# Mamba layer of a four-layer hybrid: in 4 of 16 channel pairs the scan's inputs go through ScalarE and GpSimd, and its decays stay in PSUM

## The chip, the cores and the metric

The kernel runs on one core of a Trainium2 chip. A core has a tensor engine (PE, which does matmuls into PSUM), a vector engine (DVE), a scalar engine (ACT, ScalarE), GpSimd (POOL) and a sync engine (SP) that issues the DMAs here. Each works through its own list of instructions in order, and they wait for one another through semaphores. The metric is the device time of one execution, in microseconds (us).

## The reference, cut to what matters

A tensor x of 4 images, 56 x 56 positions, 128 channels passes four layers: neighbourhood attention, Mamba, additive attention with experts, and dense attention with experts. The change lies in the second, the Mamba layer. It treats every image row as a sequence of 56 steps and runs two blocks one after the other:

```python
u = silu(conv4(h @ in_w[:, :256]));  res = h @ in_w[:, 256:]     # 256 channels
dt, Bm, Cm = split(u @ xw, [8, 24])                              # 8, 16, 16
delta = softplus(dt @ dtw + dtb);  A = -exp(A_log)               # A: 256 x 16 states
dA  = exp(delta[t, d] * A[d, n])                                 # the decays
dBu = delta[t, d] * u[t, d] * Bm[t, n]                           # the inputs
h_t = dA * h_{t-1} + dBu;  y[t, d] = sum_n h_t[d, n] * Cm[t, n] + D * u
out = (y * silu(res)) @ ow
```

So for each of 256 channels and 16 states there is a scan over time, with decays dA and inputs dBu.

## The kernel before, in words

`layer1` cuts an image into 7 chunks of 448 positions (8 rows of 56). A block is one chunk in one of the two Mamba blocks (l = 0 or 1): 4 images x 7 chunks x 2 = 56 blocks, in `order`: four chunks with l = 0, the same four with l = 1, then the other three likewise.

In a block, 256 channels x 16 states are 4096 scans, 128 at a time on the partitions (8 channels x 16 states), with two such groups side by side in one tile of 128 x 896. That is a *pair*; a block has 16 (`PAIRS`), and there are 896 in all. The work of a pair p:

- `decays` (L723): two matmuls with the matrix `A_pick` spread delta of 8 channels over 128 partitions and multiply by A, into the PSUM tile `a` (one buffer).
- ScalarE takes the Exp of `a` into the SBUF tile `E` (L748, three buffers).
- `spread_inputs` (L732): two matmuls with `pick` spread delta * u likewise into the PSUM tile `u` (two buffers).
- `inputs` (L753): DVE multiplies `u` in place, in PSUM, by B (`bc[:, 0]`).
- `scan` (L760): DVE scans over time with E (SBUF) and u (PSUM) into the SBUF tile `hs` (seven buffers). The decay at a row's first position is 0, because delta there was set very large (L939), so that rows don't mix.
- POOL multiplies `hs` in place by C (L765).
- `sums` (L771): PE adds up the 16 states into the PSUM tile `y`, for two pairs at once, in odd steps, up to five steps later.

The order on PE, ScalarE, DVE and POOL is that of the program text: `manual_schedule` leaves it as written. The main loop goes over p; what one pass issues is this:

```python
for step in first.get(p, []): step()
if p >= -2: select(p + 1)            # decays of p+2, inputs of p+1, Exp of p+2
if 0 <= p < n_pairs: scan(p)
if p % 2 and 0 <= p - 5 < n_pairs: sums(p - 5)
for step in last.get(p, []): step()
inputs(p + 1)
```

`first` and `last` hold the rest of the work, placed at fixed passes of the 16 of a block. The preparation of the next block (`mamba_pre`) is spread over the present one: convolution matmuls (L889) in passes 14, 15, 0 and 1, their copies out of PSUM (L897) first in passes 0 and 2; both Silu (L901) last in pass 2, which needs another activation table and so costs a table load before and one after; the projection to dt, B, C (L907) in pass 3; its copy (L913) and four spreading matmuls (L918) in passes 4 to 7 with their copies (L924, L929); the Softplus (L932), again between two table loads, last in pass 6; delta * u on POOL (L936) in pass 8; the residual branch (L943, L951) in passes 9 to 11. The end of a block lies in the next: the gate (L786 on ScalarE, L787 on POOL) in pass 11 and in pass 3 of the next block, the output projection (L796 for l = 0, L804 for l = 1) last in pass 8, and its copy to h (L814) or addition to X (L820, DVE) in pass 9. At three of the four images' ends, group-norm work for the next image is put in as well (L184, L194 to L229, L247).

What the change touches is `select`, `inputs` and the loop.

Of the kernel before, what the change touches and what calls it, by code (L numbers as in the profile page):

```python
# [11 lines left out]
AF = mybir.ActivationFunctionType  # L12
# [8 lines left out]
P = 128  # L21
# [3 lines left out]
CH = TC * TP  # L25
# [11 lines left out]
DBL = DR + 2 * DS  # L37
QG = 4
PAIRS = DI // 16
LONG = 1.0e30  # L40

AH = 16
# [63 lines left out]
class Hybrid:  # L106
# [570 lines left out]
    def layer1(self):  # L677
# [3 lines left out]
        nc, a, tc = self.nc, self.a, self.tc  # L681
        ET = mybir.EngineType
        with ExitStack() as ctx:
            w = self.w1
            big = ctx.enter_context(tc.tile_pool(name="l1_big", bufs=1))
            sm = ctx.enter_context(tc.tile_pool(name="l1_sm", bufs=2))
            ps_m = ctx.enter_context(tc.tile_pool(name="l1_m", bufs=1, space=PSUM))
            ps_a = ctx.enter_context(tc.tile_pool(name="l1_a", bufs=1, space=PSUM))
            ps_u = ctx.enter_context(tc.tile_pool(name="l1_u", bufs=2, space=PSUM))
# [11 lines left out]
            ]  # L701
            n_pairs = PAIRS * len(order)
            h = {}
            pre, yg, E, V, HS, py = {}, {}, {}, {}, {}, {}
# [5 lines left out]
            def place(p):  # L710

                j, i = divmod(p, PAIRS)
                return j, i // 8, i // 2 % 4, i % 2 * 2


            two_banks = lambda pool, tag: self.t(pool, [P, 1024], tag)[:, 512 - CH : 512 + CH]
            halves = lambda t: t.rearrange("p (k q) -> p k q", k=2)

            def decays(p, to):
                j, f, q, r0 = place(p)  # L720
                for k in range(2):
                    own = slice((r0 + k) * HD, (r0 + k + 1) * HD)
                    nc.tensor.matmul(  # L723
                        halves(to)[:, k], w["A"][own, order[j][2], f, q, :], pre[j]["delta"][own, f],
                        start=True, stop=True,
                    )

            def spread_inputs(p, to):
                j, f, q, r0 = place(p)
                for k in range(2):  # L730
                    own = slice((r0 + k) * HD, (r0 + k + 1) * HD)
                    nc.tensor.matmul(  # L732
                        halves(to)[:, k], w["pick"][own, q, :], pre[j]["du"][own, f],
                        start=True, stop=True,
                    )

            def select(p):
                if 0 <= p + 1 < n_pairs:  # L740
                    t = two_banks(ps_a, "a")
                    decays(p + 1, t)
                if 0 <= p < n_pairs:
                    V[p] = two_banks(ps_u, "u")
                    spread_inputs(p, V[p])
                if 0 <= p + 1 < n_pairs:
                    E[p + 1] = self.t(sm, [P, 2 * CH], "E", bufs=3)
                    nc.scalar.activation(E[p + 1], t, AF.Exp)  # L748

            def inputs(p):  # L750
                if 0 <= p < n_pairs:
                    v = halves(V[p])
                    nc.vector.tensor_mul(  # L753
                        v, v, pre[p // PAIRS]["bc"][:, 0:1].to_broadcast([P, 2, CH])
                    )


            def scan(p):
                flat = self.t(sm, [P, 2 * CH], "hs", bufs=7)
                nc.vector.tensor_tensor_scan(  # L760
                    flat, E.pop(p), V.pop(p), 0.0, op0=ALU.mult, op1=ALU.add
                )
                HS[p] = halves(flat)
                bc = pre[p // PAIRS]["bc"]
                nc.gpsimd.tensor_mul(HS[p], HS[p], bc[:, 1:2].to_broadcast([P, 2, CH]))  # L765

            def sums(p):

                j, f, q, _ = place(p)
                for r in range(4):  # L770
                    nc.tensor.matmul(  # L771
                        py[j, f][r * HD : (r + 1) * HD, :], w["sum"][:, q, :], HS[p + r // 2][:, r % 2],
                        start=False, stop=(q == QG - 1),
                    )
# [51 lines left out]
            for j, block in enumerate(order):  # L826
                at = PAIRS * j
                if j and block[1:] == (0, 0):

                    g = self.group_norm(block[0], big, w["group"])  # L830
                    for c in range(NCH):
                        to = at - (5 - c // 3) * PAIRS + 11 + c % 3
                        add(last, to, g.turn, c, m)
# [30 lines left out]
            for p in range(-PAIRS - 2, n_pairs + PAIRS):  # L864
                for step in first.get(p, []):
                    step()
                if p >= -2:
                    select(p + 1)
                if 0 <= p < n_pairs:
                    scan(p)  # L870
                if p % 2 and 0 <= p - 5 < n_pairs:
                    sums(p - 5)
                for step in last.get(p, []):
                    step()
                inputs(p + 1)

    def mamba_pre(self, pre, j, block, h, w, sm, m):

# [55 lines left out]
        def du():  # L934
# [3 lines left out]
            for f in range(NHALF):  # L938
                nc.gpsimd.memset(seqs(r["delta"][:, f])[:, :, 0:1], LONG)  # L939

# [996 lines left out]
```

## Time and profile before

| | |
|---|---|
| time, median of 3 runs | 7885.04 us (7883.99 to 7885.86) |
| span of the profiled execution, first to last instruction | 7883.1 us |
| what the median has beyond that span | 1.9 us |
| Mamba stage, first to last scan | 650.8 to 3531.3 us |
| DVE scans L760 | 896, mean 2020 ns |
| DVE products L753 | 896, mean 1076 ns |
| ScalarE Exp L748 | 896, mean 917 ns |
| POOL products L765 | 896, mean 2084 ns |
| mean granted TensorE clock, whole span | 0.949 of full speed |

The profile shows one execution. An engine's busy time is the sum of its instructions' durations; a group's line gives busy time and mean duration, then the idle time of the engine just before those instructions and what ended most of it. A timeline line is start, duration, engine, line, operation, output <- inputs, shapes, count, and in brackets the idle time before it and its releaser. A windows line is a stretch, its length, the busy time (and instructions) of PE, PE's weight loads, DVE, ACT and POOL, the granted TensorE clock, and the share and rate of the DMA.

### The profile page before, as it was taken

The numbers are of one execution on the slowest core, as the hardware profiler recorded it, in microseconds if no ns is written. First come the engines' busy times: TensorE is split into PE (matmuls) and PEld (weight loads), VectorE is DVE, ScalarE is ACT, GpSimd is POOL, SyncE is SP. The second block draws the span as 40 slices with busy tenths as digits, with TensorE's granted clock in tenths as the row PEclk, the third lists the DMA queues.
The fourth block names the chain that finished last, engine by engine and source line by source line (L and its number), as shares of the span: only waits on it lengthen the run. The fifth ranks groups of instructions, "written<-read, shape, count | busy, mean of one in ns | idle before, by whom it ended". The sixth has DMA issues, their size and how long they took to land.

```text
span 7883.1 us, 105890 instructions
## 1 busy us (share of the span) xinstructions
PE 6718.3 (85%) x41081; PEld 2672.6 (34%) x41081; DVE 6070.7 (77%) x10241; ACT 4990.0 (63%) x4903; POOL 2552.6 (32%) x1911
## 2 busy tenths in 40 slices
PE   7888989998999899987777777777777889999999
PEld 3452333333333333322222222222222344444544
DVE  5787999999999999997877887877787755344434
ACT  4455555555555655548998899899889953333332
POOL 4455777777777777760000000000001000000000
PEclk8998999999999999999999999899999989999999
DMA  3000000000000000000000000000003101210000
GB/s 63 6 2 1 1 1 1 1 1 1 1 1 1 1 1 1 1 3 2 1 1 1 5 1 1 1 5 1 1 32 114 47 6 47 91 57 5 5 5 6
DMA packets 86479, 102.35 MB, mean 13 GB/s; under 512 B 21368, under 2 KB 51414, under 8 KB 85463
## 3 DMA queue, kind: packets, MB, share of 16 engines
q1 hardware_dynamic: 85975, 95.58, 4.2%
q8 instruction: 322, 5.28, 0.3%
q14 instruction: 182, 1.49, 0.1%
HBM read 85.28 MB, written 10.29 MB: 12 GB/s over the span
## 4 chain that ended last, share of the span: by engine, by line
PE 35%; DVE 33%; ACT 20%; issue 7%; POOL 1%; DVEq 0%; DMA 0%; ACTq 0%; SPq 0%; POOLq 0%
DVE hs L760 17%; ACT th L1149 13%; PE q L1707 7%; PE o L1718 7%; DVE u L753 6%; PE s L1160 6%; DVE th L1140 4%; PE o L1187 2%; PE pe L1872 2%; ACT E L748 2%; PE a L723 2%; PE m L889 2%; DVE e L488 1%; ACT L748 1%; PE y L771 1%
## 5 line engine op out<-in xcount | busy, mean ns | idle before, releaser
L1149 ACT ACTIVATE th<-th 128x3136 f32<-128x3136 f32 (+12 forms) x1120 | 2293.6, 2093 | 194.6 <-DVE th L1140 138.4
L1140 DVE TENSOR_SCALAR th<-fT,g 128x784 f32<-128x784 f32 (+6 forms) x3920 | 1918.4, 556 | 482.2 <-PE s L1160 449.9
L765 POOL TENSOR_TENSOR hs<-hs,bc 128x896 f32<-128x896 f32 x896 | 1867.3, 2084 | 793.5 <-DVE hs L760 761.3
L1160 PE MATMUL s<-th,place 128*32 128x392 f32 (+7 forms) x14336 | 1489.2, 492 | 667.8 <-ACT th L1149 664.8
L760 DVE TENSOR_TENSOR_SCAN hs<-E,u 128x896 f32<-128x896 f32 x896 | 1810.1, 2020 | 117.9 <-ACT E L748 1.9
L748 ACT ACTIVATE E<-a 128x896 f32<-128x896 f32 x896 | 821.5, 917 | 806.3 <-PE u L732 333.7
L723 PE MATMUL a<-delta,A_pick 32*128 32x448 f32 x3584 | 983.2, 601 | 148.0 <-ACT E L748 140.4
L753 DVE TENSOR_TENSOR u<-u,bc 128x896 f32<-128x896 f32 x896 | 964.2, 1076 | 63.9 <-PE u L732 63.5
L732 PE MATMUL u<-du,pick 32*128 32x448 f32 x3584 | 975.2, 601 | 35.8 <-DVE hs L760 35.7
L1160 PEld LDWEIGHTS s<-th,place 128*32 128x32 f32 (+1 forms) x14336 | 425.7, 111 | 1612.1 <-ACT th L1149 1082.4
L1712 ACT ACTIVATE e<-q,shift 128x448 f32<-128x448 f32 (+1 forms) x700 | 441.4, 633 | 748.6 <-PE q L1707 748.2
L1178 POOL TENSOR_TENSOR e<-e,later 112x112 f32<-112x112 f32 x112 | 80.2, 716 | 2311.9 <-ACT e L1171 1670.1
L1718 PE MATMUL o<-e,xk 128*128 128x448 f32 (+1 forms) x1400 | 653.1, 548 | 25.7 <-ACT oT L1693 25.7
L1877 DVE SCALAR_TENSOR_TENSOR X<-pe,r_gate,X 112x128 f32<-112x128 f32 x896 | 314.0, 351 | 455.3 <-PE pe L1872 419.7
L1707 PE MATMUL q<-xT 128*128 128x448 f32 (+1 forms) x1400 | 654.7, 550 | 2.3 <-ACT e L1712 2.2
L723 PEld LDWEIGHTS a<-delta,A_pick 32*128 32x128 f32 x3584 | 295.7, 188 | 697.4 <-ACT E L748 466.5
L771 PE MATMUL y<-hs,sum 128*32 128x448 f32 x3584 | 443.9, 566 | 4.4 <-POOL hs L765 4.4
L1187 PE MATMUL o<-e,xa 112*128 112x392 f32 (+5 forms) x1024 | 424.3, 537 | 1.1 <-POOL e L1178 1.1
L1718 PEld LDWEIGHTS o<-e,xk 128*128 128x128 f32 (+1 forms) x1400 | 262.2, 191 | 310.5 <-issue 275.5
L732 PEld LDWEIGHTS u<-du,pick 32*128 32x128 f32 x3584 | 295.5, 188 | 200.0 <-DVE hs L760 183.9
L1707 PEld LDWEIGHTS q<-xT 128*128 128x128 f32 (+1 forms) x1400 | 249.0, 189 | 238.1 <-issue 213.0
L1806 POOL MEMSET lc_xa<- 112x4 f32 x28 | 3.1, 110 | 889.5 <-DVE lc_xa L1800 519.5
(254 smaller groups left out, 7186.2 us busy)
## 6 DMA issues: line engine op xcount, KB each, us to landing
wide<-in_L_ffn_weight SPq DMA_DIRECT2D x64, 1024.0 KB
X<-in_x SPq DMA_DIRECT2D x8, 784.0 KB
out<-X SPq DMA_DIRECT2D x28, 224.0 KB
M<-wide SPq DMA_DIRECT2D x4, 784.0 KB
wide<-M SPq DMA_DIRECT2D x4, 784.0 KB
e_edge<-dtab SPq DMA_DIRECT2D x42, 49.0 KB
cw<-in_L_conv_conv_w SPq DMA_DIRECT2D x4, 256.0 KB
c_h<-in_L_ffn_weight SPq DMA_DIRECT2D x16, 64.0 KB
```

Of the source, the lines that this page charges most:

```text
L723: nc.tensor.matmul(halves(to)[:, k], w["A"][own, order[j][2], f, q, :], pre[j]["delta"][own, f], start=True, stop=True,)
L732: nc.tensor.matmul(halves(to)[:, k], w["pick"][own, q, :], pre[j]["du"][own, f], start=True, stop=True,)
L748: nc.scalar.activation(E[p + 1], t, AF.Exp)
L753: nc.vector.tensor_mul(v, v, pre[p // PAIRS]["bc"][:, 0:1].to_broadcast([P, 2, CH]))
L760: nc.vector.tensor_tensor_scan(flat, E.pop(p), V.pop(p), 0.0, op0=ALU.mult, op1=ALU.add)
L765: nc.gpsimd.tensor_mul(HS[p], HS[p], bc[:, 1:2].to_broadcast([P, 2, CH]))
L1140: nc.vector.tensor_scalar(th[i][:, blk, lo:hi], fT[j][:, lo:hi], im[order[j][0]]["g"][:, at : at + 1], None, op0=ALU.add,)
L1149: nc.scalar.activation(own, own, AF.Tanh)
L1160: nc.tensor.matmul(ps[j, J][QW * blk : QW * blk + rows, h, lo:hi], place[:, off : off + rows], z[:, blk, h * HALF + lo : h * HALF + hi], s ...
L1187: nc.tensor.matmul(po[j][:, h, lo:hi], im[b]["xa"][:, J, :], e[:, h * HALF + lo : h * HALF + hi], start=(J == 0), stop=(J == t + ((h + 1) ...
L1707: nc.tensor.matmul(ps[:n, :CH], xT[b][:, k : k + n], xT[b][:, c * CH : (c + 1) * CH], start=True, stop=True,)
L1718: nc.tensor.matmul(po[b, c], xk[b][:n, t, :], es.pop((b, c, t))[:n], start=(t == 0), stop=(t == N - 1))
```

## The change

For the pairs 0, 3, 7 and 12 of every block (`POOL_PAIRS`) the two PSUM tiles change their contents. The pair's inputs go, one pass earlier than before, into `a`; ScalarE copies them to a new SBUF tile `V` (two buffers), and POOL multiplies V by B. Its decays go, one pass later than before, into `u`; ScalarE takes their Exp in place, in PSUM, and the scan reads them there, with V as its inputs. In ScalarE's order that Exp stands before the copy or Exp of the following pair; in POOL's order the product stands before the C product of the pair scanned in that pass. The other 12 pairs are as before.

```diff
+POOL_PAIRS = (0, 3, 7, 12)
...
+            on_pool = lambda p: p % PAIRS in POOL_PAIRS
+
             def select(p):
-                if 0 <= p + 1 < n_pairs:
+                far, near = p + 1, p
+                if 0 <= far < n_pairs:
                     t = two_banks(ps_a, "a")
-                    decays(p + 1, t)
-                if 0 <= p < n_pairs:
-                    V[p] = two_banks(ps_u, "u")
-                    spread_inputs(p, V[p])
-                if 0 <= p + 1 < n_pairs:
-                    E[p + 1] = self.t(sm, [P, 2 * CH], "E", bufs=3)
-                    nc.scalar.activation(E[p + 1], t, AF.Exp)
-
-            def inputs(p):
-                if 0 <= p < n_pairs:
+                    (spread_inputs if on_pool(far) else decays)(far, t)
+                if 0 <= near < n_pairs:
+                    u = two_banks(ps_u, "u")
+                    (decays if on_pool(near) else spread_inputs)(near, u)
+                    if on_pool(near):
+                        E[near] = u
+                        nc.scalar.activation(u, u, AF.Exp)
+                    else:
+                        V[near] = u
+                if 0 <= far < n_pairs:
+                    if on_pool(far):
+                        V[far] = self.t(sm, [P, 2 * CH], "V")
+                        nc.scalar.copy(V[far], t)
+                    else:
+                        E[far] = self.t(sm, [P, 2 * CH], "E", bufs=3)
+                        nc.scalar.activation(E[far], t, AF.Exp)
+
+            def inputs(p, eng):
+                if 0 <= p < n_pairs and on_pool(p) == (eng is nc.gpsimd):
                     v = halves(V[p])
-                    nc.vector.tensor_mul(
+                    eng.tensor_mul(
                         v, v, pre[p // PAIRS]["bc"][:, 0:1].to_broadcast([P, 2, CH])
                     )
...
                     select(p + 1)
+                    inputs(p + 2, nc.gpsimd)
...
-                inputs(p + 1)
+                inputs(p + 1, nc.vector)
```

## The prediction

> **What bounds the kernel now.** I read the engine totals first, then the groups of instructions, then the scan stage alone, then its timeline block by block. The page (its last column is idle time and who ended it):
>
> ```profile
> span 7883.1 us, 105890 instructions
> ...
> L765 POOL TENSOR_TENSOR hs<-hs,bc 128x896 f32<-128x896 f32 x896 | 1867.3, 2084 | 793.5 <-DVE hs L760 761.3
> ...
> L760 DVE TENSOR_TENSOR_SCAN hs<-E,u 128x896 f32<-128x896 f32 x896 | 1810.1, 2020 | 117.9 <-ACT E L748 1.9
> L748 ACT ACTIVATE E<-a 128x896 f32<-128x896 f32 x896 | 821.5, 917 | 806.3 <-PE u L732 333.7
> ...
> L753 DVE TENSOR_TENSOR u<-u,bc 128x896 f32<-128x896 f32 x896 | 964.2, 1076 | 63.9 <-PE u L732 63.5
> ```
>
> The Mamba stage is the 896 pairs (56 blocks of 16), from 650 to 3531 us. Its windows row (busy time of each engine, then the granted TensorE clock):
>
> ```profile
> 650.00:3531.00 2881.00, 2621.89 (x13355) 906.74 (x13354) 2742.93 (x1876) 1616.29 (x1968) 2103.30 (x1202) 0.96 0.00 1
> ```
>
> DVE is busy 95%, so it looks like the bound; but PE is busy 91%. The reader should distrust both shares and look for the loop that closes from one block to the next. I call "step p" the loop pass that selects pair p+1 and scans pair p, counted 0 to 15 in a block. The timeline of one block, PE first; the bracket is idle time before:
>
> ```profile
> 1537.70 1.02 PE L723 MATMUL a<-delta,A_pick 32*128 32x448 f32 x4 [1.00 <-ACT E L748]
> ...
> 1540.81 1.77 PE L907 MATMUL m<-us,xw 128*128 128x448 f32 x4 [0.49 <-ACT us L901]
> 1543.04 0.64 PE L723 MATMUL a<-delta,A_pick 32*128 32x448 f32 x2 [0.46 <-ACT E L748]
> ...
> 1555.22 0.65 PE L723 MATMUL a<-delta,A_pick 32*128 32x448 f32 x2 [1.22 <-ACT E L748]
> ...
> 1556.18 1.77 PE L796 MATMUL m<-yg,ow 128*128 128x448 f32 x4
> ```
>
> From step 2 to step 8 PE waits for ScalarE, whose order there is: E, table load, two silu, table load, E (steps 2 and 3); E, table load, softplus, table load, E (steps 6 to 8):
>
> ```profile
> 1536.73 0.92 ACT L748 ACTIVATE E<-a 128x896 f32<-128x896 f32 x1 [0.33 <-PE u L732]
> 1537.67 1.28 ACT L901 ACT_TABLE_LOAD   x1
> ...
> 1549.34 0.92 ACT L748 ACTIVATE E<-a 128x896 f32<-128x896 f32 x1
> 1550.27 1.28 ACT L932 ACT_TABLE_LOAD   x1
> ```
>
> And another block, where the same projection ran at half the granted clock (3.16 us, not 1.77) and DVE then waited for pair 10:
>
> ```profile
> 778.82:782.23 3.41, 3.41 (x8) 1.28 (x11) 3.28 (x3) 0.80 (x1) 2.46 (x2) 0.50 0.00 0
> ```
> ```profile
> 778.59 3.16 PE L796 MATMUL m<-yg,ow 128*128 128x448 f32 x4
> ```
> ```profile
> 783.07 1.10 DVE L753 TENSOR_TENSOR u<-u,bc 128x896 f32<-128x896 f32 x1 [0.30 <-PE u L732]
> ```
>
> Taking start times in the timeline for every block, the loop from the step-2 matmuls of one block (1535.67 above) to those of the next is a sum of five parts:
> - step 2 to step 8 on PE and ScalarE: 19.55 us in 52 of 55 blocks, 20.20 in three;
> - step 8 to pair 10's u in PSUM (the projection lies here): 3.70 to 3.93 us at full clock, on average 5.60 where the clock was 0.5;
> - slack until DVE starts pair 10's product: 0.1 or 1.0 to 2.1;
> - DVE from there to the end of scan 14: 15.80 (five pairs at 3.14);
> - scan 14's end to the next step 2: 0.05, then 9.83 of PE (L732, L771, L889 back to back).
>
> With slack 1.36: 19.55 + 3.70 + 1.36 + 15.80 + 0.05 + 9.83 = 50.29, the measured period, which is 16 x 3.14: DVE is the bound. Of the 43 blocks without group-norm work, 25 (all with a slow projection) have slack 0.1 and last 51.09; 18 have 1.49 and last 50.65; mean 50.91. So two bounds are about equally tight: DVE, and a loop PE - ScalarE - PE - DVE - PE.
>
> **The change, part by part**, for the pairs 0, 3, 7, 12 of each block.
>
> *DVE product removed, 4 a block.* Scan to scan is now 3.14 us; without the product a scan can follow at 1.94 (start to start, the distance at which a product follows a scan in the rows) plus 0.03: 1.17 saved each, 224 x 1.17 = 262 us if DVE alone mattered. Which of these count? Only pair 12 lies in the DVE part of the loop (pairs 10 to 14): -1.17. Pair 0 comes after scan 14, where PE needs 9.83 us while DVE's three pairs took 9.42 already: nothing. Pairs 3 and 7 lie between steps 2 and 8, where PE and ScalarE set the pace; DVE arrives earlier at pair 10 and waits there. That is the slack, 1.49 us in the 18 blocks, nothing in the 25.
>
> *Exp of the near pair added on ScalarE, 4 a block.* PSUM to PSUM has no row here; I bound it by 0.83 (start to start of back-to-back rows of that width) and 0.95 (L901, SBUF to SBUF); a gain is excluded, since it is one more instruction on an engine that works in order. I take 0.92, the E row, nearest in function and shape: the next one starts 0.83 later. The changed program's order on ScalarE puts it ahead of E and of the table load in step 2 (pair 3) and step 6 (pair 7). In step 2, E moves by 0.83, and with it the table load, silu, L907, everything to step 8. In step 6 ScalarE has 0.19 us idle to give: +0.64. Together +1.47 on the 19.55. In step 11 (pair 12) it moves a(14) by 0.8, but u(13) is ready 0.7 before DVE wants it; in step 15 (pair 0) E(17) ends 0.7 before PE wants its bank. Both free; without that cover they cost up to 0.8 more a block.
>
> *Copy of the far pair's inputs in place of an Exp.* L951 copies half the width in 0.53, so between 0.53 and 1.06; I take 0.90 like E: nothing changes, no table load is added (Copy runs between E rows already).
>
> *Product on POOL added.* 2.08 by L765. POOL per block: 16 x 2.084 + 2.09 + 2 x 1.13 + 0.3 = 38.0, new 46.3 of about 51. Each V product stands in POOL's queue before the preceding C product, so behind it wait those products and, four steps later, PE's sums. Pair 12's: the copy ends 3.8 to 4.4 after pair 10's u is ready (where E of pair 12 ends now, in the two kinds of block), the product at 5.9 to 6.5, scan 11 at 6.5 to 6.7: in time by 0.2 to 0.6. Pairs 0, 3, 7 by 0.5 or more. I take 0; if POOL ran 0.1 us longer per product the lag of six would cost up to 0.6.
>
> *Matmuls* are exchanged, not added, on the same row groups as now; no DMA is touched. *Scan* with its decays in PSUM and inputs in SBUF: no row; the rows reach 1.959 to 2.023, I take 2.02, +-0.06. DVE and POOL each read one SBUF tensor as before; L765 is 2071 to 2111 ns over all 896 beside a DVE 95% busy. [...]
>
> *Sum per block.* Unhindered: 50.65 - 1.49 + 1.47 - 1.17 = 49.46, plus 0.3 in the half of the blocks with L796 (pair 11 then waits for h: 16.10 in the rows, not 15.80), mean 49.6. With the slow projection: 51.09 + 1.47 - 1.17 = 51.39. The share of slow projections decides. Slow stretches follow stretches in which PE idled (above, 0.50 right after the 1.2 us wait), and the change adds 0.83 and 0.64 us of such idling, so I expect more than 25 of 43; I take 85%: 51.12, +0.21 x 43 = +9. [...]
> Slow steps 3 and 4, not seen now, would cost 0 to 0.8 a block (L907 1.77 longer, less the 0.49 and 0.46 that PE waits around it); nearest to none today, so 0.1 taken: +5. The 12 group-norm blocks: in nine PE is 0.4 to 2.1 late behind scan 14, so pair 12's gain is partly lost: +0.8 x 12 = +10. The last block has no successor and is DVE's: -4. Total +20: 7883.1 + 20 = 7903 for the span, and with the 1.9 us by which the median exceeds the span, **7905**.
>
> **Rivals.**
> 1. *DVE bound throughout*: -262 us, 7623. For it: 95% busy. Against: the slack list; DVE already stops at pair 10 in 25 of 43 blocks.
> 2. *Faster (other side)*: the new rhythm leaves the half-clock stretches away from the projection. At none: 43 x (49.6 - 50.91) = -56, +10, -4: 7835; it decides from a share under about 45%. For it: runs of blocks without one (1316 to 1513). Against: more PE idling.
> 3. *Nothing measurable*: the share stays 25 of 43: 50.65, -11, +10, -4: 7880.
> 4. *Much slower*: POOL's lag reaches the scans or steps 3 and 4 run at half clock: +0.6 to 0.8 a block, 7930 to 7955.
>
> **How the numbers follow.** Forecast (share 70 to 100%) 0.42, rival 1 0.02, rival 2 0.20, rival 3 0.22, rival 4 0.14. 0.2% is 16 us, about what a measurement can tell here. The forecast's own range, 7890 to 7925, crosses that line (7901): a sixth of its chance, 0.07, counts as same. Of rival 3, 0.20 is same and 0.02 faster. Faster 0.02 + 0.20 + 0.02 = 0.24, same 0.27, slower 0.35 + 0.14 = 0.49. The range: 7850 (rival 2 nearly whole) to 7950 (rival 4).
>
> **What would show it.** Right: DVE's idle time before L760 and L753 rises together from 182 to about 440 us, at pairs 4, 5 and 10; DVE about 2500 us busy in the stage, POOL 2570; step 2 to step 8 near 21.0; PE idle before L723 for ScalarE up by about 80 us. Wrong: a step 2 to step 8 still at 19.6, or a period near 46 us. The prediction falls if the near Exp finds idle time I missed, or if the clock's half-speed stretches change their number.

## The result, and the profile after

The changed kernel takes 7937.02 us (median; 7936.14 to 7937.26), the kernel before 7885.45 us (7883.99 to 7893.94) in the same comparison: a ratio of 1.0064, with a 95% interval of 1.0049 to 1.0078. It is slower by 51.6 us where the prediction said 20. That is inside the predicted range, but above the forecast's own 7890 to 7925, among the times that rival 4 had (7930 to 7955).

The page of the changed kernel: the span, then the groups that answer to those shown of before (mean ns of one instruction, then the engine's idle time just before, and who ended it).

```profile
span 7935.0 us, 106227 instructions
...
L778 POOL TENSOR_TENSOR hs<-hs,bc 128x896 f32<-128x896 f32 x896 | 1847.7, 2084 | 80.9 <-DVE hs L773 76.9
L773 DVE TENSOR_TENSOR_SCAN hs<-E,u 128x896 f32<-128x896 f32 x672 | 1357.7, 2020 | 68.8 <-DVE u L766 1.4
L724 PE MATMUL a<-delta,A_pick 32*128 32x448 f32 x2688 | 765.5, 614 | 290.9 <-ACT E L761 278.8
...
L766 DVE TENSOR_TENSOR u<-u,bc 128x896 f32<-128x896 f32 x672 | 727.4, 1082 | 278.2 <-PE u L733 276.8
...
L766 POOL TENSOR_TENSOR V<-V,bc 128x896 f32<-128x896 f32 x224 | 466.8, 2084 | 246.7 <-ACT V L758 246.2
L773 DVE TENSOR_TENSOR_SCAN hs<-u,V 128x896 f32<-128x896 f32 x224 | 449.9, 2008 | 88.2 <-ACT u L752 88.0
...
L752 ACT ACTIVATE u<-u 128x896 f32<-128x896 f32 x224 | 202.0, 902 | 219.1 <-PE u L724 209.5
```

Its windows row for the Mamba stage (length, busy time of PE, weight loads, DVE, ACT and POOL, then the granted TensorE clock):

```profile
644.60:3573.00 2928.40, 2505.17 (x13354) 857.68 (x13352) 2532.69 (x1653) 1787.31 (x2191) 2538.36 (x1425) 0.94 0.00 1
```

DVE has 210 us less work in the stage than before, and the stage is 48 us longer (2928.4 against 2880.6 us). DVE's idle time before its products and scans went from 182 to 435 us (68.8 + 278.2 + 88.2), and most of it ends with PE's `u`. (Some 45 us on either side is a single wait, before the stage's first pair.) No DVE wait of weight names POOL. PE's wait for `E` doubled, 140 to 279 us.

The loop of five parts, mean of the 43 plain blocks, from start times in the timelines:

| | step 2 to 8 | 8 to u(10) | slack | product 10 to end of scan 14 | to next step 2 | period |
|---|---|---|---|---|---|---|
| before | 19.55 | 4.86 | 0.69 | 15.92 | 9.88 | 50.91 |
| after | 21.40 | 5.41 | 0.14 | 14.65 | 9.77 | 51.37 |

The 12 group-norm blocks went from 53.48 to 55.94. So 43 x 0.46 = 20 and 12 x 2.46 = 30 us came in the blocks; with the edges of the stage (the last block is 2 us shorter) that is its 48 us, and all else in the program adds 4. That 4 is not explained: the part behind the stage, the same code in all of them, lasts 4350 to 4372 us in the profiles of the fourteen kernels here.

Step 2 to step 8 takes 21.29 us in the 40 blocks with a slow projection, 1.74 more than before; in the other three steps 3 and 4 ran at half clock (there L921 took 3.35 or 3.36 us instead of 1.77), and they raise the mean to 21.40. Where the 1.74 us came from, in one block's timeline (start, duration, engine, line; in brackets idle time before and its releaser). PE first, from step 3 to the projection:

```profile
1545.63 0.65 PE L724 MATMUL a<-delta,A_pick 32*128 32x448 f32 x2 [1.87 <-ACT E L761]
...
1548.73 1.77 PE L921 MATMUL m<-us,xw 128*128 128x448 f32 x4 [1.18 <-ACT us L915]
...
1559.10 0.64 PE L724 MATMUL a<-delta,A_pick 32*128 32x448 f32 x2 [0.89 <-ACT E L761]
...
1565.23 3.17 PE L809 MATMUL m<-yg,ow 128*128 128x448 f32 x4
```

ScalarE in the same block, steps 2 and 6:

```profile
1543.85 0.90 ACT L752 ACTIVATE u<-u 128x896 f32<-128x896 f32 x1 [0.39 <-PE u L724]
1544.67 0.91 ACT L761 ACTIVATE E<-a 128x896 f32<-128x896 f32 x1
1545.60 1.28 ACT L915 ACT_TABLE_LOAD   x1
...
1557.32 0.90 ACT L752 ACTIVATE u<-u 128x896 f32<-128x896 f32 x1 [0.18 <-PE a L724]
1558.13 0.91 ACT L761 ACTIVATE E<-a 128x896 f32<-128x896 f32 x1
1559.07 1.28 ACT L946 ACT_TABLE_LOAD   x1
```

The near Exp (L752) stands ahead of E and of the table load both times. PE's wait for E in step 2 is 1.87 where before had 1.00. In step 6 the near Exp itself waits, by the profile, for matmuls into the other tile, `a` (0.18 us, in 55 of the 56 blocks): the matmuls of the two tiles are interleaved and the last of `a` are late (they alternate with L932), so ScalarE's idle time, which I had counted as cover, isn't there.

And DVE, which waits at pairs 3, 5, 9 and 10:

```profile
1544.86 2.02 DVE L773 TENSOR_TENSOR_SCAN hs<-u,V 128x896 f32<-128x896 f32 x1 [0.66 <-ACT u L752]
...
1552.09 1.10 DVE L766 TENSOR_TENSOR u<-u,bc 128x896 f32<-128x896 f32 x1 [2.09 <-PE u L733]
...
1565.37 1.10 DVE L766 TENSOR_TENSOR u<-u,bc 128x896 f32<-128x896 f32 x1 [1.92 <-PE u L733]
...
1569.45 1.10 DVE L766 TENSOR_TENSOR u<-u,bc 128x896 f32<-128x896 f32 x1 [0.86 <-PE u L733]
```

The projection L809 took 3.17 us, not 1.77. Windows rows of that stretch: PE was busy 1.67 of 3.42 us, and the next stretch, with the projection, was granted 0.50.

```profile
1561.25:1564.67 3.42, 1.67 (x10) 0.60 (x10) 2.11 (x2) 3.10 (x5) 3.42 (x3) 1.00 0.01 2
1564.67:1568.08 3.41, 3.41 (x8) 1.17 (x4) 2.60 (x2) 0.92 (x1) 3.23 (x4) 0.50 0.00 0
```

This holds in 40 of the 43 plain blocks, against 25 before.

### The profile page after: what moved, and what is told of

The parts are those of the page before. It is cut to its first block, busy times and chain, and to the rows that moved or that the text cites. A ratio compares the mean times of both kernels' runs of the same rounds, so it can differ in the third digit from the quotient of the medians.

```text
span 7935.0 us, 106227 instructions
## 1 busy us (share of the span) xinstructions
PE 6600.8 (83%) x41081; PEld 2622.1 (33%) x41081; DVE 5859.5 (74%) x10017; ACT 5163.7 (65%) x5127; POOL 2989.2 (38%) x2135
## 4 chain that ended last, share of the span: by engine, by line
PE 52%; ACT 27%; DVE 13%; issue 7%; DMA 0%; POOL 0%; ACTq 0%; DVEq 0%; SPq 0%; POOLq 0%
ACT th L1163 13%; PE q L1721 7%; PE o L1732 7%; PE a L724 6%; PE s L1174 6%; DVE th L1154 5%; PE m L903 5%; ACT E L761 4%; PE o L1201 3%; PE pe L1886 2%; PE y L784 2%; DVE e L489 2%; PE a L733 2%; ACT u L752 2%; ACT L761 2%
## 5 line engine op out<-in xcount | busy, mean ns | idle before, releaser
L1174 PE MATMUL s<-th,place 128*32 128x392 f32 (+8 forms) x14336 | 1494.1, 494 | 672.0 <-ACT th L1163 668.8
L778 POOL TENSOR_TENSOR hs<-hs,bc 128x896 f32<-128x896 f32 x896 | 1847.7, 2084 | 80.9 <-DVE hs L773 76.9
L773 DVE TENSOR_TENSOR_SCAN hs<-E,u 128x896 f32<-128x896 f32 x672 | 1357.7, 2020 | 68.8 <-DVE u L766 1.4
L724 PE MATMUL a<-delta,A_pick 32*128 32x448 f32 x2688 | 765.5, 614 | 290.9 <-ACT E L761 278.8
L766 DVE TENSOR_TENSOR u<-u,bc 128x896 f32<-128x896 f32 x672 | 727.4, 1082 | 278.2 <-PE u L733 276.8
L761 ACT ACTIVATE E<-a 128x896 f32<-128x896 f32 x672 | 615.4, 916 | 375.5 <-PE u L733 363.7
L733 PE MATMUL u<-du,pick 32*128 32x448 f32 x2688 | 758.0, 615 | 5.4 <-DVE hs L773 5.3
L766 POOL TENSOR_TENSOR V<-V,bc 128x896 f32<-128x896 f32 x224 | 466.8, 2084 | 246.7 <-ACT V L758 246.2
L773 DVE TENSOR_TENSOR_SCAN hs<-u,V 128x896 f32<-128x896 f32 x224 | 449.9, 2008 | 88.2 <-ACT u L752 88.0
L724 PEld LDWEIGHTS a<-delta,A_pick 32*128 32x128 f32 x2688 | 228.2, 189 | 750.1 <-ACT E L761 534.8
L752 ACT ACTIVATE u<-u 128x896 f32<-128x896 f32 x224 | 202.0, 902 | 219.1 <-PE u L724 209.5
```

The costliest lines, as they stand in the source:

```text
L724: nc.tensor.matmul(halves(to)[:, k], w["A"][own, order[j][2], f, q, :], pre[j]["delta"][own, f], start=True, stop=True,)
L733: nc.tensor.matmul(halves(to)[:, k], w["pick"][own, q, :], pre[j]["du"][own, f], start=True, stop=True,)
L761: nc.scalar.activation(E[far], t, AF.Exp)
L766: eng.tensor_mul(v, v, pre[p // PAIRS]["bc"][:, 0:1].to_broadcast([P, 2, CH]))
L773: nc.vector.tensor_tensor_scan(flat, E.pop(p), V.pop(p), 0.0, op0=ALU.mult, op1=ALU.add)
L1174: nc.tensor.matmul(ps[j, J][QW * blk : QW * blk + rows, h, lo:hi], place[:, off : off + rows], z[:, blk, h * HALF + lo : h * HALF + hi], s ...
```

## The experiments

My theory: in this change only pair 12's product lies on the loop and gains; the near Exps of pairs 3 and 7 lengthen the loop between steps 2 and 8; and the idle time that they give PE costs clock. Rivals: a product is worth 1.17 us of DVE wherever it stands; POOL's new work costs; the near Exp costs wherever it stands; the clock has no part. Times are given with the median of the kernel before on the same chip. A pair "moved" has its inputs go through ScalarE and POOL, as in the change.

### Each pair's part: p12, p37, p0

```diff
-POOL_PAIRS = (0, 3, 7, 12)
+POOL_PAIRS = (12,)
```

and likewise (3, 7) in p37 and (0,) in p0.

> Only pair 12 of each block takes the new route; 0, 3 and 7 are as before. Loop theory (the block's period is a loop PE - ScalarE - PE - DVE - PE, only pairs 10 to 14 lie in its DVE part, and an Exp ahead of a table load in steps 2 and 6 lengthens it): step 2 to step 8 stays 19.55 us, the DVE part falls from 15.9 to about 14.5, the plain block from 50.9 to about 49.7, the whole to 7820 to 7840 us, faster than before. POOL theory (the products on POOL are too late and hold everything up): a quarter of the loss, about 7898. DVE theory (DVE is the bound throughout): 56 x 1.2 us less, 7818, so this run tells the loop from POOL, not from DVE.

> Only pairs 3 and 7 take the new route. Loop theory: both added Exps (+1.74 us a block between step 2 and step 8) and no gain in the DVE part: step 2 to step 8 21.3, plain block about 52.6, whole 7960 to 7990 us, slower than the full change although half of it is left out. DVE theory: 112 products less on DVE, 131 us less, 7754. POOL theory: half of the full change's loss, about 7911.

> Only pair 0 by the new way. Loop theory: its product lies beside PE's 9.83 us behind scan 14, off the loop; blocks with a slow projection keep 51.1, blocks with slack (DVE's bound) lose up to 1.2 us each, until they too reach the loop's 49.7 to 51.1: 0 to -25 us, 7858 to 7883, and step 2 to step 8 stays at 19.55. Rival 1 (a product less on DVE is worth the same wherever it stands, as pair 12's was): -65 us, 7815 to 7825. Rival 2 (each moved pair brings a near Exp that costs 0.9 us a block): +40 us, 7920.

| moved | time, us | before | ratio (95%) | step 2 to 8 | u(10) late | product 10 to scan 14 | plain period |
|---|---|---|---|---|---|---|---|
| 12 | 7819.39 | 7882.98 | 0.9921 (0.9907-0.9936) | 19.57 | 23 of 43 | 14.62 | 49.56 |
| 3, 7 | 8013.22 | 7882.98 | 1.0168 (1.0153-1.0183) | 22.06 | 22 of 43 | 15.87 | 53.07 |
| 0 | 7876.87 | 7886.21 | 0.9989 (0.9980-0.9998) | 19.58 | 30 of 43 | 15.92 | 50.76 |

("u(10) late": the stretch from step 8 to u(10) is above 5 us, as with a slow projection.) The three differences, -64, +130 and -9, add up to +57; the whole change has +52. That the sums are so close is in part luck: by parts the three runs add up to 0.66 us a plain block and 0.59 a group-norm block, where the whole change has 0.46 and 2.46, and half clock falls in other places in each of them. Still, the change is a gain (12), a larger loss (3 and 7) and next to nothing (0), and each lies in the part of the loop that the theory names: a product less on DVE is worth 1.3 us a block at pair 12, nothing between steps 2 and 8, and 0.15 at pair 0. For pairs 3 and 7 the loss was more than I expected, since in 18 of the 43 blocks steps 3 and 4 ran at half clock too, as in the first one, at the projection to dt, B and C (windows rows, then its matmuls, 2.39 instead of 1.77 us):

```profile
708.50:711.91 3.41, 1.54 (x19) 0.33 (x11) 3.28 (x3) 3.01 (x4) 3.30 (x3) 1.00 0.01 2
711.91:715.32 3.41, 2.99 (x14) 1.02 (x11) 3.31 (x3) 3.37 (x5) 3.08 (x2) 0.50 0.00 0
```
```profile
714.03 2.39 PE L921 MATMUL m<-us,xw 128*128 128x448 f32 x4 [0.42 <-ACT us L915]
```

### Without POOL: nopool

The change with V weighted on DVE, just ahead of its scan, instead of on POOL:

```diff
-                if 0 <= p < n_pairs and on_pool(p) == (eng is nc.gpsimd):
+                if 0 <= p < n_pairs and eng is nc.vector:
```

> The full change, but DVE makes the product V x B of pairs 0, 3, 7 and 12 in SBUF, at the place where it makes the others; POOL gets nothing new. Loop theory: step 2 to step 8 stays 21.3, the DVE part goes back to about 15.9, plain block 52.6, whole 7980 to 8010 us. POOL theory: with POOL relieved the loss goes, 7885 or less.

8009.97 us against 7882.98, ratio 1.0168 (1.0151 to 1.0185). POOL's products are not the loss: giving them back to DVE costs another 73 us (some of it half clock at steps 3 and 4, in 17 of the 43 blocks). The stretch from product 10 to scan 14 is back at 15.93, and with it the plain period at 53.24, nearly that of pairs 3 and 7 alone. This run also showed a second effect. Its V product is the only large DVE product here with both inputs in SBUF, and POOL's C product is longer in this kernel alone (its group, then one case in the timelines of POOL and of DVE):

```profile
L778 POOL TENSOR_TENSOR hs<-hs,bc 128x896 f32<-128x896 f32 x896 | 2023.5, 2258 | 721.8 <-DVE hs L773 666.3 <-PE u L733 33.4 <-PE m L185 8.0
```
```profile
1551.29 2.78 POOL L778 TENSOR_TENSOR hs<-hs,bc 128x896 f32<-128x896 f32 x1 [1.33 <-DVE hs L773]
```
```profile
1551.06 1.07 DVE L766 TENSOR_TENSOR V<-V,bc 128x896 f32<-128x896 f32 x1
```

Of the 896 POOL products the 673 that meet no such DVE product take 2.084 us, the 223 that do take 2.785. DVE's own takes 1.067: it came first each time. The scans of the changed kernel have one SBUF input (V) and one in PSUM, and there POOL's product stays at 2084 ns, as predicted (2.08 us).

### The clock: after_busy, before_busy, p12_busy, p12_busy3

Filler matmuls put PE to work where it would wait. They multiply a piece of the identity into 64 spare columns of the PSUM bank that holds `y`; nothing reads them.

```diff
+            def keep_busy(n):
+                for _ in range(n):
+                    nc.tensor.matmul(
+                        spare[0][:, CH:], self.ident, self.ident[:, : 512 - CH], start=False, stop=False
+                    )
...
+                if j:
+                    add(last, at + 2, keep_busy, 10)
+                    add(last, at + 6, keep_busy, 5)
+                    add(last, at + 7, keep_busy, 9)
```

These numbers (10, 5, 9) are those of after_busy (the changed kernel) and p12_busy3 (pair 12 alone); before_busy and p12_busy have 6 behind step 2, none behind step 6 and 8 behind step 7.

> The full change, with spare matmuls (64 columns of an identity, results unused) that keep PE busy while it waits for ScalarE: 10 after step 2's matmuls, 5 after step 6's, 9 after step 7's. Clock theory (the projection runs at half clock because PE idled just before): the projection takes 1.77 us in nearly all blocks, step 8 to pair 10's u falls from 5.4 to 3.8, plain block 49.7, whole 7850 to 7870 us. If the half clock has another cause or does not count: 7937 to 7960.

> The kernel before with only the filler matmuls added (6 behind step 2's matmuls and 8 behind step 7's in each block but the first). Clock theory (the slow projection is what makes 25 of the 43 plain blocks of before last 51.09 instead of about 50.3, and PE's idling is what makes it slow): the stretch from step 8 to pair 10's u falls from a mean of 4.86 us to 3.7 to 3.9, slack returns, plain blocks 50.3 to 50.9; time 10 to 20 us below the kernel before, 7863 to 7875. Rival (the fillers help by themselves, whatever the clock does, or after_busy won by something else): no change or slower, 7883 to 7900. If the gain here is as large as that of after_busy over the changed kernel (72 us), the half clock is no part of the change's loss; if it is a fifth of it, most of the loss was half clock that the change brought.

> Only pair 12 by the new way, with the same filler matmuls as before_busy. Loop theory: pair 12 alone ran with zero slack in the blocks with a slow projection (49.6) and with slack in the others (48.94 or 49.54, which is DVE's own 15 products and 16 scans); with the projection always at full clock all plain blocks are at DVE's bound, 48.9 to 49.6, so 10 to 25 us below pair 12 alone: 7795 to 7812. Rival (what pair 12 gains is DVE's time only and PE has no part): the same as pair 12 alone, 7815 to 7825.

> Pair 12 with fillers as in the run of the changed kernel: 10 behind step 2's matmuls, 5 behind step 6's, 9 behind step 7's (those of the earlier filler runs of pair 12 and of before were 6 behind step 2's and 8 behind step 7's, none behind step 6's). Clock theory: the 14 blocks of pair 12 with fillers that lasted 54.6 instead of 49 had their slow stretch begin in steps 5 to 7, where only a quarter of the array is in use, and the fillers of step 7 then ran at half clock themselves and lengthened it; with step 6 filled too these blocks vanish: 48.9 to 49.6 throughout, 7790 to 7812. Rival (fillers are dead weight on PE, the clock is not governed by them): 7850 or more, worse than 49.2 a block by the added 3 to 4 us of filler time.

| | time, us | before | ratio (95%) | half clock in the stage, us | u(10) late | plain period |
|---|---|---|---|---|---|---|
| before | | | | 222 | 25 of 43 | 50.91 |
| change | 7937.02 | 7885.45 | 1.0064 (1.0049-1.0078) | 375 | 40 of 43 | 51.37 |
| after_busy | 7865.23 | 7882.98 | 0.9976 (0.9966-0.9986) | 61 | none | 50.21 |
| before_busy | 7888.29 | 7886.21 | 1.0003 (0.9993-1.0012) | 137 | 7 of 43 | 51.56 |
| p12 | 7819.39 | 7882.98 | 0.9921 (0.9907-0.9936) | 182 | 23 of 43 | 49.56 |
| p12_busy | 7849.23 | 7886.21 | 0.9956 (0.9943-0.9969) | 256 | 14 of 43 | 51.09 |
| p12_busy3 | 7802.23 | 7887.11 | 0.9890 (0.9876-0.9905) | 51 | none | 49.33 |

The stage of after_busy, and its projection in a block:

```profile
648.10:3498.40 2850.30, 2665.31 (x15994) 1115.92 (x15992) 2529.41 (x1653) 1792.47 (x2191) 2541.09 (x1425) 0.99 0.00 1
```
```profile
1544.00 1.77 PE L817 MATMUL m<-yg,ow 128*128 128x448 f32 x4
```

So the changed kernel, with 2640 matmuls more on PE, is 72 us faster (difference of the medians): half clock costs it more than the change loses. Part of the 72 was there before: in before_busy, below, the undisturbed plain blocks last 50.69 on average, 43 x 0.22 = 9 us less than before's, and the group-norm blocks 52.34 instead of 53.48, 14 us; and the same fillers took only 17 us off the kernel with pair 12 alone. So the larger part is half clock that the change brought; before with these same fillers was not run. Step 2 to step 8 stays at 21.31, so the near Exps still cost their 1.74 us; with u(10) no longer late, DVE has 0.75 us of slack again. The group-norm blocks are back at 53.47, before's mean, though the near Exps stand in them too, so much of what they lost was half clock as well. That isn't so everywhere: the three at an image's end are still 9 us longer together than in the kernel before, the other nine 9 us shorter.

before_busy and p12_busy missed. In their undisturbed blocks the theory holds (step 8 to u(10) 4.1, plain periods mostly 50.28 or 50.88, and 48.94 or 49.54). But 7 and 14 blocks lasted 5.4 us longer, in one slow stretch of 13.65 us. It began in step 7 ahead of its fillers, behind a step 6 without any, and those of step 7 then ran at half clock, 16 matmuls in 3.68 us where 18 took 2.22 in a block of p12_busy3; that they made it longer is my reading (windows rows of p12_busy, and two of PE's lines in it):

```profile
817.02:820.44 3.42, 3.40 (x18) 1.05 (x18) 3.16 (x4) 3.27 (x4) 2.35 (x2) 1.00 0.00 0
820.44:834.09 13.65, 13.65 (x50) 6.56 (x46) 8.24 (x6) 4.59 (x7) 9.30 (x7) 0.50 0.00 0
```
```profile
821.80 3.68 PE L800 MATMUL y<-ident 128*128 128x64 f32 x16
...
828.69 3.35 PE L817 MATMUL m<-yg,ow 128*128 128x448 f32 x4
```

PE was busy 3.40 of the 3.42 us ahead of the slow stretch, so idling is not the whole rule: those were nearly all matmuls on 32 rows or 32 columns of the array. p12_busy3 was made to test that, with fillers behind step 6 too (and four more behind step 2, one more behind step 7, so step 6 is not tested by itself): no block is late any more, every plain block lasts 48.9 to 49.9 us, and 7802 is within what the clock theory gave (7790 to 7812).

### More pairs of the same kind: p10_13_busy, p12_14, p0_12_14, p0_12_busy3

If the loop theory says which pairs pay, it should find a better set. p10_13_busy has the fillers of before_busy, p0_12_busy3 those of p12_busy3.

```diff
-POOL_PAIRS = (0, 3, 7, 12)
+POOL_PAIRS = (10, 13)
```

and likewise (12, 14), (0, 12, 14) and (0, 12).

> Pairs 10 and 13 by the new way, both in the DVE part of the loop (product of pair 10 to the end of scan 14), with the fillers. Loop theory: two products leave that part, 2 x 1.2 us a block, and no near Exp falls between steps 2 and 8 (they stand in steps 9 and 12): step 2 to step 8 stays at 19.55, plain blocks 47.6 to 48.4, 43 x -2.8 and 12 x -2: 7725 to 7770, the fastest of all. Rival (ScalarE's or POOL's new work costs wherever it stands, about 10 us for each pair moved): 7860 or more.

> Pairs 12 and 14 by the new way, no fillers. Loop theory: both products lie between pair 10's product and the end of scan 14, and the near Exps stand in steps 11 and 13, where ScalarE carries little else and PE waits for no copy behind them (that of pair 10, in step 9, stood ahead of the copy to h): step 2 to step 8 19.55, the DVE part 13.3 to 13.5, plain blocks 47.8 (DVE's bound, 16 x 3.14 - 2 x 1.2) to 48.4 (loop with a slow projection): 43 x -2.8 and 12 x -1.7 on before: 7735 to 7765. Rival (a second pair gains nothing, as in the run with pairs 10 and 13): 7815 to 7830.

> Pairs 0, 12 and 14. Loop theory: pair 0 is worth something only where a block has slack; with 12 and 14 out of the DVE part the loop (46.6 at full clock, 48.2 with a slow projection) and DVE (46.6) are about equal, so the gain over pairs 12 and 14 is 0 to 1.2 us in the blocks with slack: 0 to -40 us on that run. Rival (each pair costs a near Exp): +10 to +40.

> Pairs 0 and 12 with the fillers behind steps 2, 6 and 7 (10, 5, 9). With pair 12 and these fillers every plain block was DVE's (48.94 or 49.53) with slack 0.61 or 0.96 ahead of pair 10's product. Loop theory: pair 0 takes 1.2 us from DVE but lies off the loop, so the gain is exactly the slack down to its floor of 0.1: -0.5 and -0.87 us a block, plain blocks 48.4 and 48.7, some -30 us on that run: 7765 to 7785. Rival 1 (a product less on DVE is worth 1.2 us wherever it stands, while DVE is the bound): -55 to -65, 7735 to 7750. Rival 2 (pair 0's near Exp in step 15 costs PE time behind scan 14): 7800 or more.

| moved | time, us | before | ratio (95%) |
|---|---|---|---|
| 10, 13, fillers | 7824.35 | 7886.21 | 0.9922 (0.9907-0.9937) |
| 12, 14 | 7836.93 | 7887.11 | 0.9935 (0.9918-0.9952) |
| 0, 12, 14 | 7841.05 | 7887.11 | 0.9938 (0.9923-0.9953) |
| 0, 12, fillers | 7791.29 | 7883.68 | 0.9886 (0.9870-0.9903) |

All four missed their expectation, p0_12_14 by no more than the noise: a second pair gains little or nothing over pair 12, because another wait closes the loop first. In p10_13_busy five plain blocks also lasted 54.8 us, as the slow ones of p12_busy did; the others last 49.14. With pair 10 its near Exp stands in step 9 ahead of the copy to `h`, and PE waits 1.41 us for that (without the near Exp, 0.54 in the runs with pair 12). ScalarE, then PE:

```profile
876.32 0.90 ACT L752 ACTIVATE u<-u 128x896 f32<-128x896 f32 x1 [2.05 <-PE u L724]
877.13 0.91 ACT L761 ACTIVATE E<-a 128x896 f32<-128x896 f32 x1
877.93 0.54 ACT L835 COPY h<-m 128x448 f32<-128x448 f32 x1
```
```profile
878.53 1.02 PE L968 MATMUL m<-h,res_w 128*128 128x448 f32 x2 [1.41 <-ACT h L835]
```

With pairs 12 and 14 it is POOL, for the first time in this study: after V(12) two C products and the gate stand ahead of V(14), which was copied out at 1542.55, and scan 14 waits 1.96 us. POOL, then DVE:

```profile
1539.74 4.12 POOL L778 TENSOR_TENSOR hs<-hs,bc 128x896 f32<-128x896 f32 x2
1543.82 1.14 POOL L800 TENSOR_TENSOR yg<-yg,sres 128x448 f32<-128x448 f32 x1
1544.92 2.07 POOL L766 TENSOR_TENSOR V<-V,bc 128x896 f32<-128x896 f32 x1
```
```profile
1547.02 2.02 DVE L773 TENSOR_TENSOR_SCAN hs<-u,V 128x896 f32<-128x896 f32 x1 [1.96 <-POOL V L766]
```

Adding pair 0 to those two gave no gain that the intervals can tell (0.9938 against 0.9935): scan 0 then waits for POOL's V as well, 0.98 us in the median. With pairs 0 and 12 and the fillers, plain blocks fell from 48.94 and 49.54 to 48.86 and 49.46, where I expected 48.4 and 48.7: DVE, 1.2 us earlier, now waits 0.81 us at pair 5 for PE. The fillers are not needed for that: with pair 0 alone, which has none, it waits there as long (DVE of p0):

```profile
1537.71 1.10 DVE L766 TENSOR_TENSOR u<-u,bc 128x896 f32<-128x896 f32 x1 [0.80 <-PE u L733]
```

The median, 7791, is the lowest measured, but its interval and that of p12_busy3 overlap. Both beat the kernel before by 1.1%, and the changed kernel by more.

## Why the prediction was right, and by how much it was off

- *The loop of two bounds* held: DVE's 95% was no bound, DVE lost 210 us of work and the stage grew. Rival 1 (7623) was far off. The time is one that rival 4 had, but neither of its conditions was met: POOL's lag held up no scan, and steps 3 and 4 ran at half clock in 3 plain blocks only.
- *DVE's idle time* 182 to about 440: measured 435, though at pairs 5, 9 and 10 and at the scan of pair 3 (40 us, waiting for the near Exp), not at 4, 5 and 10. That the sum came out is in part luck: DVE's work fell by 210 us where 243 was said, and the stage grew by 48 where 20 was. Both 182 and 435 hold the wait before the stage's first pair, 45.35 us before its product in the kernel before, and in the changed kernel:

```profile
644.59 2.02 DVE L773 TENSOR_TENSOR_SCAN hs<-u,V 128x896 f32<-128x896 f32 x1 [45.93 <-ACT u L752]
```

- *DVE's and POOL's busy time* 2500 and 2570: 2533 and 2538.
- *Near Exp +1.47* was too small: 1.74, of it 0.88 in step 2 (0.83 said) and 0.86 in step 6 (0.64 said). The duration was right (0.90 us for 0.92); the cover of 0.19 us in step 6 was not there, because the near Exp also waits for the matmuls of the other tile. PE's idle time for E rose by 138 us, not 80.
- *Pair 12 -1.17*: -1.27 in the block means (15.92 to 14.65), and -64 us in the run that moves it alone. *Pair 0 nothing*: -9 us. *Pairs 3 and 7 gain nothing*: shown by the run that moves them alone.
- *V on POOL 0*: right for the scans of these four pairs, but not for the group norm's small DVE work at an image's end (below). The lag that rival 4 named came only with pairs 12 and 14.
- *The share of slow projections, 85%*: 93%. The rise from PE's added waits was argued in the prediction and is shown by the fillers. *Slow steps 3 and 4, 0.1 a block*: that term was my own estimate, and no run shows it by itself. The changed kernel had slow steps 3 and 4 in 3 of 43 plain blocks (above 22 us), which fits it, but with pairs 3 and 7 alone it was 18 of 43; I had no means of telling which.
- *Group-norm blocks +10*: the term that failed most, +29.5 measured. The three at an image's end gave 6.6 each and the other nine 9.7 together; the nine late ones that I spoke of include those three. At an image's end PE waits longer for the group norm than before, 2.24 us for 0.73, and two convolutions ran at half clock, where in the kernel before one did in two of these three blocks and none in the third (PE's lines of one of them, before and after):

```profile
1982.60 0.38 PE L205 MATMUL m<-gn_dev,group 128*128 128x1 f32 x2 [0.73 <-DVE gn_dev L213]
```
```profile
2002.36 0.38 PE L206 MATMUL m<-gn_dev,group 128*128 128x1 f32 x2 [2.24 <-DVE gn_dev L214]
...
2005.44 3.22 PE L903 MATMUL m<-h,in_w 128*128 128x448 f32 x4
```

In sum: plain blocks +20 where +9 and +5 were said, group-norm blocks +30 for +10, the rest of the program +4, the last block -2 for -4. The step that was mis-sized is the last, by 20 of the 32 us. Rival 2 named the right mechanism for the other side: without slow projections the change is a gain (after_busy, on the kernel before as it is), of 18 us instead of the 50 it gave; that the near Exps cost more is part of the difference.

## What to carry to other kernels

Where two bounds are about equal, find for each instruction that is removed or added the part of the loop in which it lies: the same edit gained 64 us at one pair, nothing at another and lost 130 at two more. Ask who waits behind an instruction that is put ahead of others on its engine: the same Exp cost 0.86 to 0.88 us in steps 2 and 6, where it stands ahead of a table load that PE waits behind, while with that of pair 12 in step 11, or of pair 0 in step 15, the kernel got faster all the same. Look for half-clock stretches when PE waits regularly: filling those waits with work nobody reads took 72 us off this kernel, but fewer fillers gained nothing on the kernel before and cost 30 us with pair 12.

## What was not expected of the hardware

*The granted clock followed work more closely than busy time.* In the trace's clock record the slow stretches of a run all start on one grid of 3.413 us and last a multiple of it (but for one that the end of the record cuts off). I counted the matmuls that start in each such window of the stage as rows x columns x streamed columns, in units of 128 x 128 x 448; the fullest windows hold 8. In the kernel before, full-clock windows that are followed by a slow one hold 2.0 to 4.0 (44 windows, median 3.1), those followed by full clock 6.0 in the median, and 95% of them 3.75 or more (733). The other thirteen runs look much the same: never more than 4.25 ahead of a slow window, a median of 5.75 to 6.0 otherwise. PE's busy time tells the two kinds apart less well: in the kernel before it is 1.38 to 3.39 us ahead of a slow window (median 2.20), and 65% of the others lie in that range too. Little work is not the whole rule either: of the windows of the kernel before with 4.25 or less, 44 were followed by half clock and 131 by full clock. But a window full of quarter-array matmuls was followed by half clock though PE was busy 3.40 of 3.42 us; the one shown above holds 3.75. Nor does it take an idle window: of the 576 windows ahead of a slow one in the fourteen runs, three held no matmul's start, and the fullest held 4.25 of the 8.

*Blocks settle on that grid.* 35 of the 43 plain blocks of the changed kernel last 51.22 to 51.35 us, and 15 windows are 51.20: each block meets the window at the same phase, so its projection is slow again. That the slow stretch causes this, rather than the two sums being close by chance, is argued and not shown.

*A product of 128 x 1 can take 2 us.* In the changed kernel's stage 12 of DVE's group-norm products, with both inputs in SBUF, start while a POOL product runs; they last 0.84 to 2.01 us, and each ends 0.013 to 0.018 us after that POOL product. This one started at 2000.12 and POOL's, from 2000.03, ended at 2002.10 (DVE, then POOL):

```profile
2000.12 1.99 DVE L213 TENSOR_TENSOR gn_dev<-gn_dev 128x1 f32<-128x1 f32 x1
```
```profile
2000.03 2.07 POOL L778 TENSOR_TENSOR hs<-hs,bc 128x896 f32<-128x896 f32 x1
```

Undisturbed such a product takes 0.16, as the same line did there in the kernel before:

```profile
1982.18 0.16 DVE L212 TENSOR_TENSOR gn_dev<-gn_dev 128x1 f32<-128x1 f32 x1
```

With POOL busier in the changed kernel, the group-norm instructions on DVE sum to 35.1 us in the stage instead of 27.6, all of it in the three blocks at an image's end. The scans with V, which have one input in PSUM, show nothing like it (2008 ns in the mean, for 2020 before), but the small work beside them does. And PE waits for that work: its 2.24 us at the group norm, shown in the section on the prediction, end with this chain of products. The wait comes with pair 12, whose V product is new work for POOL just there: with pair 12 alone it is 1.9 to 2.2 us, with pairs 3 and 7 alone 0.5 to 0.7. after_busy has the same 35.1 us and the same wait, and its three blocks are the ones that are still 9 us longer than in the kernel before. How much of the 20 us that these three lost comes from this wait, how much from the near Exps and how much from half clock behind it was not separated.
